# A four-layer graph network on one core: layer 1's first rows as a pipeline over four engines, and the end of layer 2 taken in steps beside layer 3

## The chip, the core and the metric

The kernel runs on one core of one Trainium2 chip. The time is the device time in microseconds of the core, median of the runs. Five engines work beside each other, each in its own program order: TensorE (PE in the profile; its weight loads are PEld), VectorE (DVE), ScalarE (ACT), GpSimd (POOL) and SyncE (SP, which issues transfers here). In the code they are `T`, `V`, `S`, `G` and `nc.sync`.

## What is computed

`x` has 4096 rows of 64, `adj` is a 4096 x 4096 matrix of zeros and ones, sparse. Four layers follow one another, each on the layer norm of `x` with its negative part cut off, and each adds its result to `x`:

```python
h = relu(layernorm(x)); x = x + layer0(h, adj)      # hyperbolic attention over the neighbours
h = relu(layernorm(x))
deg = clip(sum(adj, 1) + 1, 1)                      # layer 1
z = relu(concat([h, (adj @ h + h) / deg]) @ W1 + b1)
x = x + z / max(norm(z), 1e-12)
h = relu(layernorm(x))
for k in range(2):                                  # layer 2: two hops
    h = tanh(concat([adj @ h, h], 1) @ W2[k])
x = x + h
h = relu(layernorm(x))                              # layer 3
w = mask(adj) * 0.5 ** (how many neighbours stand to the right in the row), the last 100 of a row
x = x + w @ (h @ W3) + b3
```

The kernel multiplies by the weights first: `y = h @ W`, then `adj @ y`. Each `y` is split into three bf16 parts (value, rest, rest of the rest) that stand side by side, so a product with the 0/1 adjacency in fp8 has 3 x 64 columns and loses nearly nothing.

## The kernel before

The 4096 rows are 32 chunks of 128 rows, one chunk per partition set; eight chunks are a group, and there are four groups. `x` is 128 x 32 x 64 in SBUF. At the end of layer 0, `finish` writes the last two groups of `x`:

```python
        yield 0.35
        for g in range(g0, g1):
            rows, part = slice(g * 8, g * 8 + 8), slice((g - g0) * 8, (g - g0) * 8 + 8)
            t, s = block(f"f_t{g}"), block(f"f_s{g}")
            V.tensor_mul(t, h[:, rows, :], bc(a[:, part], D))
            V.tensor_mul(s, vs[:, rows, :D], bc(f[:, part], D))
            yield 1.4
            V.tensor_add(s, s, t)
            V.tensor_add(x[:, rows, :], x[:, rows, :], s)
            yield 1.4
```

Layer norm of a group (128 x 8 x 64, so 512 elements in each partition), used ahead of layers 1, 2 and 3, with its root:

```python
    def root(self, pool, a, n, name):
        V, S = self.nc.vector, self.nc.scalar
# [... cut: tiles s, inv, q ...]
        S.activation(s, a, AF.Sqrt)
        V.reciprocal(inv, s)
        V.tensor_mul(q, a, inv)
        V.tensor_add(q, q, s)
        V.tensor_scalar_mul(s, q, 0.5)
        V.reciprocal(inv, s)
        return s, inv
# [... cut ...]
    def ln_group(self, pool, xx, h, name, block=None):
        V, S = self.nc.vector, self.nc.scalar
        st = pool.tile([P, 8], F32, tag="ln_st", name=f"{name}_st")
# [... cut ...]
        V.tensor_reduce(st, xx, AX.X, ALU.add)
        V.tensor_scalar_mul(st, st, 1.0 / D)
        V.tensor_sub(cen, xx, st[:, :, None].to_broadcast([P, 8, D]))
        S.activation(sq, cen, AF.Square)
        var = pool.tile([P, 8], F32, tag="ln_v", name=f"{name}_v")
        V.tensor_reduce(var, sq, AX.X, ALU.add)
        V.tensor_scalar(var, var, 1.0 / D, LN_EPS, op0=ALU.mult, op1=ALU.add)
        _, inv = self.root(pool, var, 8, name)
        V.tensor_mul(cen, cen, inv[:, :, None].to_broadcast([P, 8, D]))
        V.tensor_scalar_max(h, cen, 0.0)
```

The weight product of a group, with the splitting into three parts:

```python
    def weigh(m, h, y3, w, name, bias=None):

        nw = D if w is None else w.shape[-1]
        pt = bank("t", f"{name}_t{m}").rearrange("p (k i) -> p k i", k=4)
        for k in range(4):
            T.transpose(pt[:, k, :], h[:, 2 * k : 2 * k + 2, :].rearrange("p k d -> p (k d)"), ident)
        ht = lw.tile([P, 4, P], F32, tag="ht", name=f"{name}_h{m}")
        S.copy(ht, pt)
        if nw == D:

            pu = bank("u", f"{name}_u{m}")
            for k in range(4):
                T.matmul(pu[:, k * P : (k + 1) * P], ht[:, k, :], w3_t, start=True, stop=True)
            outs = [(pu.rearrange("p (k e) -> p k e", k=GR), slice(m * GR, m * GR + GR))]
        else:
            pus = [bank("u", f"{name}_u{m}_{s}").rearrange("p (k e) -> p k e", k=4) for s in range(2)]
            for k in range(GR):
                half = slice(k % 2 * D, k % 2 * D + D)
                T.matmul(pus[k % 2][:, k // 2, :], ht[half, k // 2, :], w[half, :], start=True, stop=True)
            outs = [(pus[s], slice(m * GR + s, m * GR + GR, 2)) for s in range(2)]
        for pu, rows in outs:
            n = pu.shape[1]
            yy = pu[:, :, :D]
            S.copy(y3[:, rows, 0:D], yy)
            rest = lw.tile([P, n, D], F32, tag=f"rest{n}", bufs=8 // n, name=f"{name}_r{rows.start}")
            V.tensor_sub(rest, yy, y3[:, rows, 0:D])
            S.copy(y3[:, rows, D : 2 * D], rest)
            V.tensor_sub(y3[:, rows, 2 * D : 3 * D], rest, y3[:, rows, D : 2 * D])
            if nw > D:
                if bias is None:
                    S.copy(base[:, rows, :], pu[:, :, D:])
                else:
                    V.tensor_add(base[:, rows, :], pu[:, :, D:], along_d(bias, n))
# [... cut ...]
    def joined(acc, agg):
        V.tensor_reduce(agg, acc[:, :, : 3 * D].rearrange("p k (s d) -> p k d s", s=3), AX.X, ALU.add)

    def product(y3, cols, name, made, tail, order, done, beside, itself=False, behind={}):


        first = [c for m in made[:-1] for c in range(m * GR, m * GR + GR)]
        last = range(made[-1] * GR, made[-1] * GR + GR)
        for at, m in enumerate(order):
            agg = lw.tile([P, GR, D], F32, tag="agg", bufs=3, name=f"{name}_agg{m}")
            accs = {}

            def part(k, chunks):
# [... cut: one T.matmul(acc, adjacency of row chunk k and chunk c, y3[:, c]) for each chunk c ...]
            def end(k):
# [... cut: with `itself` the product of the identity idb with y's own chunk; then, if k is odd: ...]
                    done(m, k // 2, accs[k // 2], agg)

            if at == 0:
                for g in made[:-1]:
                    for k in range(GR):
                        part(k, range(g * GR, g * GR + GR))
                    if g in behind:
                        behind[g]()
                tail()
                for k in range(GR):
                    part(k, last)
                    end(k)
                continue
            for k in range(GR):
                part(k, first)
                part(k, last)
                end(k)
                if k == 5:
                    beside(order[at - 1])
```

`product` multiplies the adjacency with `y` for one group of output rows after another (`order`). In the first of them the chunks of `y` are taken as the groups of `y` are made: `made`, with `behind` called after a group's products, and `tail` ahead of the last group. Then the use of it. The whole block fixes the order of instructions by hand: each engine runs them in the order written.

```python
# [... cut: tri and fill of layer 3 are made here, see the diff ...]
        hs = {}
        V.memset(y3s[0][:, :, 3 * D : 3 * D + 1], 1.0)
        dgs = {}

        def first_y(m):
            weigh(m, ln_group(m, "ln1"), y3s[0], both(0), "l1", bias=b1_t)

        first_y(0)
        first_y(1)
# [... cut ...]
        product(
            y3s[0], 3 * D + 1, "l1", up, lambda: None,
            up, l1_done, lambda m: weigh(m, hs[m], y3s[1], both(1), "l2"), itself=True,
            behind={0: lambda: first_y(2), 1: lambda: first_y(3)},
        )
# [... cut ...]
        def hop(m, k2, acc, agg):
            pair = agg[:, 2 * k2 : 2 * k2 + 2, :]
            joined(acc, pair)
            V.tensor_add(pair, pair, base[:, m * GR + 2 * k2 : m * GR + 2 * k2 + 2, :])
            if k2 == GR // 2 - 1:
                S.activation(agg, agg, AF.Tanh)
                aggs[m] = agg
                return True

        def second_y(m):
            weigh(m, aggs[m], y3s[0], both(2), "l2b")

        product(
            y3s[1], 3 * D, "l2a", up, lambda: weigh(NQ - 1, hs[NQ - 1], y3s[1], both(1), "l2"), up, hop, second_y
        )

        def l2b_done(m, k2, acc, agg):
            if hop(m, k2, acc, agg):
                V.tensor_add(x[:, group(m), :], x[:, group(m), :], agg)
                hs[m] = ln_group(m, "ln3")
                V.tensor_add(x[:, group(m), :], x[:, group(m), :], along_d(b3_t, GR))

        def third_y(m):
            weigh(m, hs[m], y3s[1], None, "l3")

        product(y3s[0], 3 * D, "l2b", up, lambda: second_y(NQ - 1), down, l2b_done, third_y)
```

Layer 3 takes the rows in four quarters (`q`) of eight chunks. For every chunk `c` of columns, from the right, `cnt` counts by TensorE how many neighbours stand to the right; a weight tile (the power of two as a bit pattern) is made from each half of it, one half on VectorE and one on ScalarE; `fill` then brings the counts on for the next chunk.

```python
        def weighted(q, accs, item):
# [... cut: eight T.matmul of the weight tiles' 128-column pieces with y3[:, c] into accs ...]

        for q in range(NQ):
            accs = [bank("acc", f"l3_acc{q}_{k}", bufs=4).rearrange("p (k e) -> p k e", k=2) for k in range(4)]
            cnt = [bank("t" if b else "u", f"cnt{q}_{b}") for b in range(2)]
            pend = None
            for c in reversed(range(NCH)):
                head_, last = c == NCH - 1, c == 0
                masks = [a8[2 * q + b][:, c, :] for b in range(2)]
                for b in range(2):
                    T.matmul(cnt[b], tri, masks[b], start=head_, stop=last, skip_group_check=True)
                wts = [lw.tile([P, 512], I16, tag=f"wt{b}", bufs=3, name=f"wt{q}_{c}_{b}") for b in range(2)]
                if pend is not None:
                    weighted(q, accs, pend)
                pend = (c, wts)
                if q == 0 and c == 22:
                    third_y(0)
                V.tensor_scalar(wts[0], cnt[0], -(128.0 - MAX_NEIGH) * UNIT, 0.0, op0=ALU.add, op1=ALU.max)
                S.activation(wts[1], cnt[1], AF.Relu, bias=low_t)
                if not last:
                    for b in range(2):
                        T.matmul(cnt[b], fill, masks[b], start=False, stop=False, skip_group_check=True)
            weighted(q, accs, pend)
            rows = slice(q * GR, (q + 1) * GR)
            agg = lw.tile([P, GR, D], F32, tag="agg", bufs=3, name=f"l3_agg{q}")
            for k2 in range(4):
                joined(accs[k2], agg[:, 2 * k2 : 2 * k2 + 2, :])
            z = lw.tile([P, GR, D], F32, tag="sq", name=f"z3_{q}")
            V.scalar_tensor_tensor(z, agg, 2.0**27, x[:, rows, :], op0=ALU.mult, op1=ALU.add)
            nc.sync.dma_start(out[:, rows, :], z)
```

## Time and profile before

| what | value |
|---|---|
| time, median of 3 runs | 947.08 us (944.4 to 957.32) |
| span of the profiled execution | 943.8 us |
| layer 0 ends, layer 1 begins | 360 us |
| layer 1's first row block ends | 422 us |
| layer 2 begins, second hop, layer 3 | 497, 598, 698 us |

The profile page has shares of busy time for each engine, the span in 40 slices, groups of instructions, and the chain of work that ended last. Beside it the trace can be asked for stretches (busy time of each engine between two times, with the clock granted to TensorE as a share of its full speed, the share of time in which the transfer engines were busy, and GB/s) and for the timeline. A line of the timeline is: start in us, length in us, engine, line of the kernel before, operation, out<-in by the names of the tiles, shapes, count, and in brackets the idle time of the engine before it and what ended it. Lines L1743 to L1752 are the layer norm, L1725 to L1732 its root, L1467 to L1494 `weigh`, L1501 `joined`, L1520 and L1529 `product`, L1649 to L1680 layer 3.

### The profile page before, as it was taken

The numbers are of one execution on the slowest core, as the hardware profiler recorded it, in microseconds if no ns is written. First come the engines' busy times: TensorE is split into PE (matmuls) and PEld (weight loads), VectorE is DVE, ScalarE is ACT, GpSimd is POOL, SyncE is SP. The second block draws the span as 40 slices with busy tenths as digits, with TensorE's granted clock in tenths as the row PEclk, the third lists the DMA queues.
The fourth block names the chain that finished last, engine by engine and source line by source line (L and its number), as shares of the span: only waits on it lengthen the run. The fifth ranks groups of instructions, "written<-read, shape, count | busy, mean of one in ns | idle before, by whom it ended". The sixth has DMA issues, their size and how long they took to land.

```text
span 943.8 us, 15045 instructions
## 1 busy us (share of the span) xinstructions
PE 770.2 (82%) x6076; PEld 576.1 (61%) x6096; DVE 518.1 (55%) x1496; ACT 343.3 (36%) x471; POOL 167.6 (18%) x178
## 2 busy tenths in 40 slices
PE   4767765986898751789998999989958989989896
PEld 1323333733637331679998999989955656656564
DVE  4668777776889976445555222144443344444443
ACT  4766566574631332211112011122223334434342
POOL 0337766176277100000000000000000000000000
PEclk9879897798998985799999899999988899999999
DMA  8889999899711006300000000000000000000000
GB/s 285 309 309 324 377 354 350 293 364 340 267 38 28 8 1 288 158 1 1 1 2 1 1 1 1 2 1 2 1 1 1 1 12 1 2 12 1 12 2 15
DMA packets 48225, 98.39 MB, mean 104 GB/s; under 512 B 6290, under 2 KB 6290, under 8 KB 47250
## 3 DMA queue, kind: packets, MB, share of 16 engines
q1 hardware_dynamic: 35232, 79.70, 23.5%
q10 hardware_dynamic: 7794, 11.98, 3.4%
q0 software_dynamic: 5120, 5.66, 2.8%
q8 instruction: 49, 0.80, 0.3%
q14 instruction: 30, 0.25, 0.1%
HBM read 84.66 MB, written 12.67 MB: 103 GB/s over the span
## 4 chain that ended last, share of the span: by engine, by line
PE 66%; DMA 12%; DVE 10%; ACT 9%; issue 2%; ACTq 0%; SPq 0%
PE l2a_acc L1520 9%; PE l2b_acc L1520 9%; PE l_acc L1649 9%; PE l_acc L1520 8%; PE cnt L1673 7%; DMA adj<-f 7%; PE cnt L1662 6%; PE fill_t L1117 4%; ACT f L796 3%; PE v L1131 3%; PE pk L801 2%; DMA a<-in_adj_t 2%; PE v L1124 2%; ACT a L793 1%; PE l_u L1480 1%
## 5 line engine op out<-in xcount | busy, mean ns | idle before, releaser
L1520 PEld LDWEIGHTS <-a 128*128 128x128 fp8e4 x3072 | 264.8, 99 | 9.2 <-issue 6.9
L1669 DVE TENSOR_SCALAR wt<-cnt 128x512 int16<-128x512 f32 x128 | 88.5, 691 | 123.4 <-PE cnt L1662 123.4
L997 POOL DMA_INDIRECT es<-rows_d,idx x128 | 126.7, 989 | 98.7 <-issue 36.3
L1670 ACT ACTIVATE wt<-cnt,low_t 128x512 int16<-128x512 f32 x128 | 88.0, 687 | 137.2 <-PE cnt L1662 137.2
L1649 PEld LDWEIGHTS <-wt 128*128 128x128 bf16 x1024 | 90.1, 99 | 31.7 <-issue 2.5
L1649 PE MATMUL l_acc<-y_b,wt 128*128 128x192 bf16 x1024 | 107.8, 249 | 0.0
L1117 PE MATMUL fill_t<-io,wpack 128*128 128x512 bf16 x298 | 93.8, 406 | 13.5 <-DVE hw L971 7.3
L1673 PE MATMUL cnt<-a,fill 128*128 128x512 fp8e4 x248 | 82.2, 387 | 20.3 <-DVE wt L1669 20.0
L1520 PE MATMUL l_acc<-y_a,a 128*128 128x193 bf16 x1024 | 93.9, 252 | 0.0
L796 ACT CAST f<-a 128x2048 fp8e4<-128x2048 f32 x40 | 75.8, 1896 | 47.5 <-DMA adj<-f 45.9
L1520 PE MATMUL l2a_acc<-y_b,a 128*128 128x192 bf16 x1024 | 89.4, 250 | 3.0 <-DVE y_b L1489 3.0
L1520 PE MATMUL l2b_acc<-y_a,a 128*128 128x192 bf16 x1024 | 88.2, 248 | 3.0 <-DVE y_a L1489 3.0
L801 PE MATMUL pk<-a,wpack 128*128 128x512 bf16 x248 | 74.1, 420 | 16.6 <-DMA a<-in_adj_t 16.1
L1662 PE MATMUL cnt<-a,tri 128*128 128x512 fp8e4 x256 | 78.0, 387 | 0.0
L1117 PEld LDWEIGHTS <-wpack 128*128 128x128 bf16 x310 | 31.3, 104 | 65.0 <-issue 36.1
L801 PEld LDWEIGHTS <-wpack 128*128 128x128 bf16 x256 | 26.9, 108 | 50.0 <-issue 17.4
L811 PE MATMUL keys<-ident,kt 128*128 128x128 f32 x64 | 14.7, 371 | 49.3 <-ACT kt L807 49.3
L793 ACT CAST a<-a 128x2048 fp8e4<-128x2048 f32 x24 | 45.0, 1898 | 12.0 <-DMA a<-in_adj_t 7.7
L1662 PEld LDWEIGHTS <-tri 128*128 128x128 bf16 x256 | 25.0, 98 | 38.2 <-issue 23.2
L811 PEld LDWEIGHTS keys<-ident,kt 128*128 128x128 f32 x64 | 9.4, 184 | 57.5 <-ACT kt L807 57.5
L1673 PEld LDWEIGHTS <-fill 128*128 128x128 bf16 x248 | 24.2, 98 | 28.0 <-issue 21.3
L1467 PE MATMUL l_t<-ident,ln_h 128*128 128x128 f32 x48 | 8.3, 301 | 38.0 <-DMA a<-adj 23.2
(376 smaller groups left out, 890.9 us busy)
## 6 DMA issues: line engine op xcount, KB each, us to landing
a<-in_adj_t SPq DMA_DIRECT2D x64, 1024.0 KB, 7.6
adj<-f ACTq DMA_DIRECT2D x40, 256.0 KB, 5.9
a<-adj SPq DMA_DIRECT2D x5, 2048.0 KB, 16.5
es<-rows_d,idx POOLq DMA_INDIRECT x128, 5.3
rows_d<-tab ACTq DMA_DIRECT2D x1, 1104.0 KB
x<-in_x SPq DMA_DIRECT2D x1, 1024.0 KB
out<-z SPq DMA_DIRECT2D x4, 256.0 KB, 2.0
es<-rows_d,ovx POOLq DMA_INDIRECT x32, 5.5
```

The source lines that it names most:

```text
L793: S.copy(a8[b][:, 4 * at : 4 * at + 4, :], a, saturate=False)
L796: S.copy(f8, a, saturate=False)
L801: T.matmul(pk, wflat[:, w * P : (w + 1) * P], bits[:, j, :, 1], start=(w == 0), stop=(w == 15),)
L997: G.indirect_dma_start(out=dst, out_offset=None, in_=rows_d, in_offset=bass.IndirectOffsetOnAxis(ap=at, axis=0))
L1117: T.matmul(fill_t, wflat[:, :P], fill_in, start=True, stop=True, skip_group_check=True)
L1131: T.matmul(pv[:, k * DQ : (k + 1) * DQ], spot[nb][:, c, k * P : (k + 1) * P], es[g][:, q, LB * NS + c, :DQ], start=False, stop=(c == NO - ...
L1520: T.matmul(acc, a8[n // 4][:, c, n % 4 * P : (n % 4 + 1) * P], y3[:, c, :cols], start=(c == first[0] and k % 2 == 0), stop=(c == last[-1] ...
L1649: T.matmul(accs[k // 2][:, k % 2, : 3 * D], wts[k // 4][:, (k % 4) * P : (k % 4 + 1) * P].bitcast(BF16), y3[:, c, : 3 * D], start=(c == NC ...
L1662: T.matmul(cnt[b], tri, masks[b], start=head_, stop=last, skip_group_check=True)
L1669: V.tensor_scalar(wts[0], cnt[0], -(128.0 - MAX_NEIGH) * UNIT, 0.0, op0=ALU.add, op1=ALU.max)
L1670: S.activation(wts[1], cnt[1], AF.Relu, bias=low_t)
L1673: T.matmul(cnt[b], fill, masks[b], start=False, stop=False, skip_group_check=True)
```

## The change

It does four things. In layer 1 the layer norms of the four groups are laid out as a pipeline: VectorE makes the sums, GpSimd centres and scales groups 1 to 3, ScalarE squares and cuts the negative part, and the weight products of groups 1 to 3 are taken in steps amid the first products with the adjacency, so that TensorE need not wait for a whole group's norm. `weigh` becomes a generator of such steps (`weighing`) and splits both halves of a group beside each other. The last group of layer 2 is closed in steps beside the first chunks of layer 3; while they run, ScalarE makes both weight tiles, and also in the first two chunks of the later quarters. At the end of layer 0 two of the last products go to GpSimd, and the set-up of layer 3's tiles moves behind layer 1. In the diff only changed lines are shown; `...` stands for unchanged ones.

```diff
--- before.py
+++ after.py
@@ -1260,7 +1260,7 @@
-            V.tensor_mul(t, h[:, rows, :], bc(a[:, part], D))
+            (G if g1 == NQ else V).tensor_mul(t, h[:, rows, :], bc(a[:, part], D))
@@ -1444,7 +1444,6 @@
-    V.tensor_copy(idb, ident)
@@ -1459,6 +1458,11 @@
+        for _ in weighing(m, h, y3, w, name, bias):
+            pass
+    def weighing(m, h, y3, w, name, bias=None):
@@ -1467,6 +1471,7 @@
+        yield
@@ -1479,19 +1484,25 @@
+        yield
+        rests = []
...
-            yy = pu[:, :, :D]
-            S.copy(y3[:, rows, 0:D], yy)
+            S.copy(y3[:, rows, 0:D], pu[:, :, :D])
...
-            V.tensor_sub(rest, yy, y3[:, rows, 0:D])
+            V.tensor_sub(rest, pu[:, :, :D], y3[:, rows, 0:D])
+            rests.append(rest)
+            if nw == D:
+                yield
+        for rest, (pu, rows) in zip(rests, outs):
...
-            if nw > D:
-                if bias is None:
-                    S.copy(base[:, rows, :], pu[:, :, D:])
-                else:
-                    V.tensor_add(base[:, rows, :], pu[:, :, D:], along_d(bias, n))
+        if nw > D:
+            for pu, rows in outs:
+                S.copy(base[:, rows, :], pu[:, :, D:])
+            if bias is not None:
+                G.tensor_add(base[:, group(m), :], base[:, group(m), :], along_d(bias, GR))
+        yield
@@ -1500,7 +1511,7 @@
-    def product(y3, cols, name, made, tail, order, done, beside, itself=False, behind={}):
+    def product(y3, cols, name, made, tail, order, done, beside, itself=False, amid={}):
@@ -1535,10 +1546,11 @@
+                    steps = amid.get(g)
...
-                    if g in behind:
-                        behind[g]()
+                        if steps is not None and k > 0:
+                            next(steps, None)
@@ -1555,27 +1567,64 @@
-        tri_f = res.tile([P, P], F32, name="tri_f")
-        tri = res.tile([P, P], BF16, name="tri")
-        fill_f = res.tile([P, P], F32, name="fill_f")
-        fill = res.tile([P, P], BF16, name="fill")
-        low_t = res.tile([P, 1], F32, name="low_t")
-        V.memset(low_t, -(128.0 - MAX_NEIGH) * UNIT)
-        V.tensor_scalar(tri_f, diff, 0.0, -UNIT, op0=ALU.is_lt, op1=ALU.mult)
-        V.scalar_tensor_tensor(tri, ident, 128.0 * UNIT, tri_f, op0=ALU.mult, op1=ALU.add)
-        V.tensor_scalar(fill_f, diff, 0.0, -UNIT, op0=ALU.is_gt, op1=ALU.mult)
-        V.scalar_tensor_tensor(fill, ident, -129.0 * UNIT, fill_f, op0=ALU.mult, op1=ALU.add)
...
-        def first_y(m):
-            weigh(m, ln_group(m, "ln1"), y3s[0], both(0), "l1", bias=b1_t)
-        first_y(0)
-        first_y(1)
+        cens = [lw.tile([P, GR, D], F32, tag="ln_h", name=f"ln1_c{m}") for m in range(2)]
+        cens += [lw.tile([P, GR, D], F32, tag="agg", bufs=3, name=f"ln1_c{m}") for m in range(2, NQ)]
+        sqs = [lw.tile([P, GR, D], F32, tag=tag, name=f"ln1_s{m}") for m, tag in enumerate(["ln_b", "ln_b", "sq", "sq"])]
+        def means(m0, m1, eng):
+            n = (m1 - m0) * GR
+            st = lw.tile([P, n], F32, tag=f"st{n}", name=f"ln1_st{m0}")
+            sum_d(st, x[:, m0 * GR : m1 * GR, :])
+            V.tensor_scalar_mul(st, st, 1.0 / D)
+            for m in range(m0, m1):
+                at = slice((m - m0) * GR, (m - m0) * GR + GR)
+                eng.tensor_sub(cens[m], x[:, group(m), :], over_d(st[:, at], GR))
+        def squares(m0, m1):
+            for m in range(m0, m1):
+                S.activation(sqs[m], cens[m], AF.Square)
+        def scales(m0, m1, eng):
+            n = (m1 - m0) * GR
+            var = lw.tile([P, n], F32, tag=f"var{n}", name=f"ln1_v{m0}")
+            for m in range(m0, m1):
+                sum_d(var[:, (m - m0) * GR : (m - m0) * GR + GR], sqs[m])
+            V.tensor_scalar(var, var, 1.0 / D, LN_EPS, op0=ALU.mult, op1=ALU.add)
+            _, inv = root(lw, var, n, f"ln1_{m0}")
+            for m in range(m0, m1):
+                at = slice((m - m0) * GR, (m - m0) * GR + GR)
+                eng.tensor_mul(cens[m], cens[m], over_d(inv[:, at], GR))
+        def relus(m0, m1):
+            for m in range(m0, m1):
+                S.activation(cens[m], cens[m], AF.Relu)
+        ys = [weighing(m, cens[m], y3s[0], both(0), "l1", bias=b1_t) for m in range(NQ)]
+        means(0, 1, V)
+        squares(0, 1)
+        means(1, 2, G)
+        scales(0, 1, V)
+        squares(1, 2)
+        relus(0, 1)
+        next(ys[0])
+        means(2, NQ, G)
+        next(ys[0])
+        scales(1, 2, G)
+        squares(2, NQ)
+        relus(1, 2)
+        for _ in ys[0]:
+            pass
+        V.tensor_copy(idb, ident)
+        scales(2, NQ, G)
+        def second_weights():
+            yield from ys[1]
+            relus(2, NQ)
@@ -1605,8 +1654,20 @@
-            behind={0: lambda: first_y(2), 1: lambda: first_y(3)},
+            amid={0: second_weights(), 1: ys[2], 2: ys[3]},
...
[... cut: the set-up of tri and fill removed above, unchanged ...]
@@ -1627,14 +1688,45 @@
+        closing = []
...
-            if hop(m, k2, acc, agg):
+            if m == 0 and k2 == GR // 2 - 1:
+                closing.append(closing_steps(m, k2, acc, agg))
+            elif hop(m, k2, acc, agg):
...
+        def closing_steps(m, k2, acc, agg):
+            rows = group(m)
+            hop(m, k2, acc, agg)
+            yield True
+            V.tensor_add(x[:, rows, :], x[:, rows, :], agg)
+            st, var = (lw.tile([P, GR], F32, tag=f"{t}{GR}", name=f"ln3_{t}") for t in ("st", "var"))
+            sum_d(st, x[:, rows, :])
+            V.tensor_scalar_mul(st, st, 1.0 / D)
+            yield True
+            cen = lw.tile([P, GR, D], F32, tag="ln_h", name="ln3_c")
+            sq = lw.tile([P, GR, D], F32, tag="ln_b", name="ln3_s")
+            V.tensor_sub(cen, x[:, rows, :], over_d(st, GR))
+            S.activation(sq, cen, AF.Square)
+            yield True
+            sum_d(var, sq)
+            V.tensor_scalar(var, var, 1.0 / D, LN_EPS, op0=ALU.mult, op1=ALU.add)
+            yield True
+            _, inv = root(lw, var, GR, "ln3")
+            V.tensor_mul(cen, cen, over_d(inv, GR))
+            yield True
+            V.tensor_scalar_max(cen, cen, 0.0)
+            V.tensor_add(x[:, rows, :], x[:, rows, :], along_d(b3_t, GR))
+            yield True
+            for _ in weighing(m, cen, y3s[1], None, "l3"):
+                yield False
@@ -1664,9 +1756,12 @@
-                if q == 0 and c == 22:
-                    third_y(0)
-                V.tensor_scalar(wts[0], cnt[0], -(128.0 - MAX_NEIGH) * UNIT, 0.0, op0=ALU.add, op1=ALU.max)
+                busy = next(closing[0], False) if q == 0 else c > NCH - 3
+                if busy:
+                    S.activation(wts[0], cnt[0], AF.Relu, bias=low_t)
+                else:
+                    V.tensor_scalar(wts[0], cnt[0], -(128.0 - MAX_NEIGH) * UNIT, 0.0, op0=ALU.add, op1=ALU.max)
```

## The prediction

> **What bounds the kernel now.** I read the page first, for the shares of the engines:
>
> ```profile
> PE 770.2 (82%) x6076; PEld 576.1 (61%) x6096; DVE 518.1 (55%) x1496; ACT 343.3 (36%) x471; POOL 167.6 (18%) x178
> ```
>
> TensorE (PE) is busiest, but 82% is a mean over stages, so I asked next for the busy time in stretches that follow the code (columns: stretch, its length, busy us of each engine, then the clock granted to TensorE).
>
> ```profile
> 374.00:382.00 8.00, 1.11 (x4) 0.71 (x4) 5.10 (x14) 1.22 (x3) 0.00 (x0) 0.50 1.03 439
> 382.00:395.00 13.00, 10.06 (x84) 9.10 (x84) 6.62 (x18) 3.01 (x8) 0.00 (x0) 0.76 0.31 132
> 395.00:409.00 14.00, 9.82 (x98) 9.04 (x100) 6.61 (x18) 2.95 (x8) 0.00 (x0) 0.87 0.00 1
> 420.00:497.00 77.00, 74.81 (x882) 73.73 (x881) 41.48 (x113) 12.79 (x33) 0.00 (x0) 1.00 0.01 2
> 694.00:716.00 22.00, 12.70 (x98) 9.07 (x96) 10.54 (x23) 7.30 (x11) 0.00 (x0) 0.77 0.00 1
> ```
>
> The reader is to see that layer 1 from 420 us on is bound by TensorE (74.81 of 77 us, clock 1.00), and that its start and the seam between layers 2 and 3 are not: there TensorE waits and then runs at half clock. So a saved wait there moves everything behind it. The timeline gives the waits:
>
> ```profile
> 380.47 1.11 PE L1467 MATMUL l_t<-ident,ln_h 128*128 128x128 f32 x4 [9.46 <-DVE ln_h L1752]
> 384.27 7.38 PE L1520 MATMUL l_acc<-y_a,a 128*128 128x193 bf16 x64
> 393.73 0.66 PE L1467 MATMUL l_t<-ident,ln_h 128*128 128x128 f32 x4 [2.08 <-DVE ln_h L1752]
> 406.59 0.66 PE L1467 MATMUL l_t<-ident,ln_h 128*128 128x128 f32 x4 [3.32 <-DVE ln_h L1752]
> ...
> 708.03 1.01 PE L1673 MATMUL cnt<-a,fill 128*128 128x512 fp8e4 x2 [9.30 <-DVE wt L1669]
> 730.43 1.01 PE L1673 MATMUL cnt<-a,fill 128*128 128x512 fp8e4 x2 [3.38 <-DVE wt L1669]
> 772.86 0.59 PE L1673 MATMUL cnt<-a,fill 128*128 128x512 fp8e4 x2 [2.44 <-DVE wt L1669]
> ```
>
> L1520 is a product with the adjacency, L1467 the transposes ahead of the weight products, L1673 the `fill` product of layer 3. Products of the first row block begin only at 384.27, although y of group 0 was ready at 374.46: by program order TensorE stands behind group 1's transposes, which wait 9.46 us for group 1's layer norm, nearly all of it on VectorE. The block ends at 422.1. At 708.03 and 730.43 `fill` waits for a weight tile that VectorE makes only after the layer norm, or the last y conversion.
>
> [...] granted 0.50 from 365 to 388 us, 0.99 in 388 to 390, that is 4 us after the products began; after the 9.3 us wait it was 0.50 until about 712. So each removed wait also removes a cold stretch.
>
> [...]
>
> ```profile
> 28.01 0.69 DVE L732 TENSOR_TENSOR cens<-cens,ln_i 128x512 f32<-128x512 f32 x1
> 30.60 1.19 POOL L738 TENSOR_TENSOR cens<-tab,wl_t 128x512 f32<-128x512 f32 x1
> 31.28 1.05 DVE L732 TENSOR_TENSOR cens<-cens,ln_i 128x512 f32<-128x512 f32 x1
> ```
>
> The VectorE product takes 0.69 us alone and 1.05 us when it meets the GpSimd one: it ends 0.54 us after GpSimd's end at 31.79. GpSimd needs 1.19 us for what VectorE does in 0.69.
>
> [...] Relu at 704.42 follows a Sqrt with no table load. So the Relus moved to ScalarE bring no loads of 1.28 us (the trace's duration).
>
> **Part 1, layer 1's start.** Walk through the new order with the trace's durations (128x512: VectorE product 0.69, reduction 0.69, GpSimd 1.19, ScalarE 0.63; about 0.05 us from engine to engine).
>
> End of layer 0: two of eight products go to GpSimd. [...] 354.5 + 6 x 0.6 (VectorE's pitch) + 2 x 1.19 = 360.5, against 359.9. I book a loss of 0.6, not a gain.
>
> Group 0: the six small instructions for `tri`, `fill` and `idb` (359.92 to 361.04) are moved away, saving 1.1. Memset, sum, scale, centring end at 362.2; square 362.85; the table load for Sqrt to 364.15; the variance's last step may be held by GpSimd's centring of group 1 to 364.4; root 365.75; scaling 366.5; Relu on ScalarE 367.15 (0.63 for VectorE's 0.43). Transposes at 367.2, as before (367.17); weight products end at 371.1 at half clock (1.1 + 0.6 + 2.1).
>
> The splitting of y0 then stands on ScalarE behind Relu of group 1. That chain: sums of groups 2 and 3 on VectorE to 367.95, variance of group 1 with GpSimd centring beside it to 369.4, [...] scaling on GpSimd 372.6, Relu 373.3. Splitting in the new order (two casts, two differences, two casts, two differences, from the trace 0.37, 0.42, 0.41, 0.43 and pitches of 0.31 to 0.35) takes 2.15: y0 is ready at 375.5. Products begin there, 8.8 us before 384.27.
>
> From there nothing should wait: each group gives eight packets of eight products, and the next group's transposes, weight products and splitting hang between the packets. y1 is ready about 9 us after the start (two packets 2.7 at half clock, transposes 1.1, packet 1.2, weight products 1.8, splitting 2.3), and group 0's packets last 10.5. TensorE's own work: 8 x 2.805 us (the pitch of 32 products plus the identity one, from 422 us on) = 22.4; three times transposes and weight products 3 x 1.76 = 5.3; half clock for about 4.5 us costs 2.3. Sum 30.0, end at 405.5, against 422.1: gain 16.6. For small unseen waits I take 16.
>
> **Part 2, the tails of layers 2a and 2b.** The new splitting order also serves the last group, on which TensorE waits alone: after the weight products end at 515.41 it does one product at 517.23 and goes on at 518.67. In the new order all is split 2.15 us after the end: 517.55. Gain 1.1, twice 2.2. If the shorter gap keeps the clock (0.50 from 518 to 524 now), there is up to 2 more; I book 0.3. Sum 2.5.
>
> **Part 3, the seam to layer 3.** Now the first Tri product is at 698.06 and that of chunk 18, where the rhythm of 1.64 us is back, at 738.36: 40.3 us for 13 chunks, whose rhythm would be 21.3. In the new order ScalarE makes both weight tiles in six chunks. First chunk: reduction, sum and Tanh end at 699.89 as now, then two Relus of 0.69: `fill` ends at 701.47, so 3.4 us. A busy chunk then runs: Tri product, 0.42 to the first Relu, two Relus to 1.75, second `fill` to 2.0. Five of them 10.0, and one holds the table load and Sqrt, of which 0.65 fits in ScalarE's gap: 0.8 more. VectorE's norm runs ahead beside this. Then the steps of the weight product: transposes with the copy ahead of the Relu on ScalarE 3.45; weight products 2.85; two splitting steps 2.1 and 1.7. Chunks 21 to 19 run at the rhythm, 4.9. Sum 3.4 + 10.0 + 0.8 + 10.1 + 4.9 = 29.2[...]. Gain 40.3 - 29.2 = 11.1; I take 10 for a clock that may dip.
>
> **Part 4, between the row quarters of layer 3.** Three times `fill` waits 2.44 us for VectorE, which sums the finished quarter first (four reductions 1.95, the addition 0.69). Now Tri to Tri is 3.46; with both tiles on ScalarE 2.05, and the next chunk 0.4 above its rhythm: gain 1.0 each, 3.0. One gap of the three now goes cold and loses about 1.4; I book 0.5. Sum 3.5.
>
> Sum: 16 + 2.5 + 10 + 3.5 = 32. From 947.1 this gives 915.
>
> **Rivals.** [...] GpSimd holds VectorE back more than I booked. Against it: only six GpSimd instructions of 1.19 us lie before the first product (two in layer 0's end, four in layer 1), and a VectorE reduction was not slowed beside one (0.69 at 30.68). If each cost its whole length once more, y0 would be 7 us later: 922. Second, ScalarE becomes the bound: its Relu of groups 1 to 3 ahead of y's casts, or both weight tiles plus the closing work in a chunk. The window 716 to 770 has it 20.94 of 54 us busy, so there is room, but order matters and not the sum. If every seam chunk took 3 us instead of 2, six us are lost: 921. Third, the adjacency's second part, in flight from 360 to 387 us, becomes the wait once products start earlier. Against: the first row block reads the resident part, and row block 1 would begin at 405, 18 us after the last byte; nothing lost. Fourth, the clock: intermittent work at the seam keeps TensorE at half speed, half of part 3 and 2 us of part 1 gone: 922. All at once would be near 935.
>
> **Range and chances.** The parts are counted from durations, so the uncertainty is in waits: I put 12 to 18 for part 1, 6 to 12 for part 3, 3 to 8 for the rest. The three runs before spread from 944.4 to 957.3, which adds some us. I expect 915 us, 905 to 926 in 8 of 10. Two per cent is 928; it takes two rivals together to miss it: 0.88 faster, 0.09 within, 0.03 slower.
>
> **What would show it.** Products of layer 1 begin 8 to 9 us earlier (about 375), their first row block ends near 405 without a wait over 1 us; VectorE instructions of 0.69 us stretch to over 1 us beside GpSimd; layer 0's end is no earlier; no `fill` wait of 9 us remains, but some ten of 0.4; quarter gaps shrink to about 1 us. I'm wrong if the row block waits for y1 or y2, if a table load stands at each seam chunk, or if the clock is 0.50 through the seam.

## The result, and the profile after

| | before | after |
|---|---|---|
| time, median of 4 runs | 945.74 us (942.31 to 957.32) | 909.66 us (905.76 to 911.43) |
| span of the profiled execution | 943.8 us | 904.0 us |

The ratio is 0.9624, 95% interval 0.9575 to 0.9674: the changed kernel is 3.8% faster. By the medians the gain is 36.1 us, by the two profiled executions 39.8; the profiled execution of after is the fastest of its four.

The page of the kernel after, shares of the engines:

```profile
PE 759.9 (84%) x6076; PEld 567.6 (63%) x6096; DVE 498.9 (55%) x1456; ACT 353.0 (39%) x494; POOL 181.5 (20%) x190
```

TensorE has the same 6076 instructions and is busy 10.3 us less: half-clock time has gone (it is busy at half clock for 98.6 us before and for 74.4 after, by the clock records of the two traces). ScalarE and GpSimd are busy 9.7 and 13.9 us longer. Where the 40 us come from is read from milestones of the two traces. All times below are counted **from the end of layer 0** (its last addition ends at 359.89 us before and 361.02 after), since layer 0's length varies by some us from run to run. A tail is the place in each hop of layer 2 where TensorE waits for the last group's `y`; the seam is the passage from layer 2 to layer 3; Tri is the product with `tri` that opens each chunk of layer 3.

| stretch | before | after | gain | booked |
|---|---|---|---|---|
| layer 0's last eight blocks of 128x512 | 5.40 | 6.01 | -0.6 | -0.6 |
| end of layer 0 to the first product of layer 1 | 24.38 | 13.35 | 11.0 | } 16.6 |
| first product to the end of the first row block | 37.86 | 29.40 | 8.5 | |
| rest of layer 1 | 74.74 | 74.74 | 0.0 | 0 |
| layer 2, first hop and second hop | 201.27 | 196.22 | 5.0 | 2.5 |
| seam: first Tri product of layer 3 to that of chunk 18 | 40.22 | 28.91 | 11.3 | 10 |
| rest of layer 3 | 205.40 | 200.32 | 5.1 | 3.5 |

The rows below the first sum to 40.9 us. The end of layer 0 lies 1.1 us later (the 0.6, and 0.5 in where those blocks begin), so the span falls by 39.8.

The kernel after in stretches (stretch, length, busy us of PE, PEld, DVE, ACT and POOL with counts, granted clock, share of transfers, GB/s):

```profile
361.00:374.00 13.00, 3.20 (x20) 2.50 (x20) 9.58 (x27) 6.93 (x14) 4.12 (x4) 0.50 0.93 376
374.00:404.00 30.00, 29.53 (x326) 28.09 (x327) 9.61 (x29) 9.53 (x27) 7.10 (x6) 0.93 0.45 189
404.00:478.00 74.00, 71.81 (x848) 70.74 (x845) 40.29 (x111) 12.57 (x33) 0.00 (x0) 1.00 0.01 2
674.00:704.00 30.00, 25.27 (x173) 16.28 (x171) 12.67 (x25) 16.39 (x26) 0.00 (x0) 0.94 0.00 1
```

From the first product to the end of the row block TensorE is now busy 29.53 of 30 us; before, its stretches there were busy 10.06 of 13 and 9.82 of 14. The stretch of layer 1 that was already bound by TensorE is unchanged. The seam is the only stretch of these where TensorE still waits after it has begun.

The timeline of the kernel after, from layer 0's end into layer 1:

```profile
355.01 0.69 DVE L1264 TENSOR_TENSOR f_s<-vs,f_f 128x512 f32<-128x512 f32 x1
355.04 2.58 POOL L1263 TENSOR_TENSOR f_t<-tab,f_a 128x512 f32<-128x512 f32 x2 [42.80 <-DVE f_f L1258]
356.65 1.52 DVE L1266 TENSOR_TENSOR f_s<-f_s,f_t 128x512 f32<-128x512 f32 x1 [0.94 <-POOL f_t L1263]
...
363.61 1.04 POOL L1586 TENSOR_TENSOR ln_c<-x,ln_st 128x512 f32<-128x512 f32 x1 [5.99 <-issue]
364.10 0.58 DVE L1597 TENSOR_SCALAR ln_v<-ln_v 128x8 f32<-128x8 f32 x1
...
369.23 2.08 PE L1485 MATMUL l_u<-wab,l_h 64*128 64x128 f32 x16 [0.67 <-ACT l_h L1473]
...
372.07 0.63 ACT L1605 ACTIVATE ln_c<-ln_c 128x512 f32<-128x512 f32 x1 [1.22 <-POOL ln_c L1601]
372.60 0.63 ACT L1491 CAST y_a<-l_u 128x256 bf16<-128x256 f32 x2
...
374.37 2.91 PE L1531 MATMUL l_acc<-y_a,a 128*128 128x193 bf16 x16 [3.06 <-DVE y_a L1499]
...
377.08 1.06 PE L1471 MATMUL l_t<-ident,ln_c 128*128 128x128 f32 x4
...
384.71 0.60 PE L1471 MATMUL l_t<-ident,ln_c 128*128 128x128 f32 x4
...
391.91 0.60 PE L1471 MATMUL l_t<-ident,ln_c 128*128 128x128 f32 x4
```

Three things are to be seen. At 356.65 VectorE's addition takes 1.52 us where the next one (359.60) takes 0.69: it runs beside the second of GpSimd's two products, which ends at 357.62, and ends 0.55 us after it. (The first took 1.57 us, beside VectorE's own product of 355.01, and the second 1.04.) At 364.10 a VectorE step on 128 x 8 values, 0.17 us at 363.31, takes 0.58 and ends 0.03 us after GpSimd's centring, which ends at 364.65. And y0 is split at 372.60 only when ScalarE has made the Relu of group 1; the first product follows at 374.37. The transposes of groups 1 to 3 (L1471 at 377.08, 384.71 and 391.91) carry no bracket: TensorE has not been idle ahead of any of them.

The timeline of the kernel after, TensorE at the seam and at the first turn between quarters:

```profile
677.11 0.38 PE L1768 MATMUL cnt<-a,fill 128*128 128x512 fp8e4 x1 [1.78 <-ACT wt L1762]
...
686.50 0.38 PE L1768 MATMUL cnt<-a,fill 128*128 128x512 fp8e4 x1 [0.63 <-ACT wt L1762]
...
692.25 0.38 PE L1768 MATMUL cnt<-a,fill 128*128 128x512 fp8e4 x1 [1.05 <-ACT wt L1765]
...
736.21 0.38 PE L1768 MATMUL cnt<-a,fill 128*128 128x512 fp8e4 x1 [0.56 <-ACT wt L1762]
736.78 0.38 PE L1768 MATMUL cnt<-a,fill 128*128 128x512 fp8e4 x1 [0.20 <-ACT wt L1765]
```

The wait of 9.30 us for VectorE's tile has become one of 1.78 in the first chunk and then several of 0.2 to 1.05, and the releaser is now ScalarE's Relu (L1762, L1765). At the turn of a quarter 2.44 us have become 0.56 and 0.20.

And the seam, cut where its clock changes, kernel after (the number ahead of the last two is the clock):

```profile
675.17:678.58 3.41, 1.43 (x9) 0.63 (x7) 2.58 (x6) 2.05 (x4) 0.00 (x0) 1.00 0.00 0
678.58:681.99 3.41, 3.41 (x17) 2.23 (x16) 1.13 (x3) 2.62 (x5) 0.00 (x0) 0.50 0.00 0
681.99:685.40 3.41, 3.21 (x25) 1.99 (x24) 0.00 (x0) 2.46 (x4) 0.00 (x0) 1.00 0.00 0
```

Here the clock falls to 0.50, and TensorE's longest gap ahead of that was 1.78 us. This comes back below.

### The profile page after: what moved, and what is told of

Same layout as the page of the kernel before. It is cut to its first block, busy times and chain, and to the rows that moved or that the text cites. A ratio compares the mean times of both kernels' runs of the same rounds, so it can differ in the third digit from the quotient of the medians.

```text
span 904.0 us, 15063 instructions
## 1 busy us (share of the span) xinstructions
PE 759.9 (84%) x6076; PEld 567.6 (63%) x6096; DVE 498.9 (55%) x1456; ACT 353.0 (39%) x494; POOL 181.5 (20%) x190
## 4 chain that ended last, share of the span: by engine, by line
PE 62%; DMA 15%; ACT 11%; DVE 8%; issue 2%; ACTq 1%; POOL 0%; DVEq 0%; POOLq 0%
DMA adj<-f 11%; PE l_acc L1531 10%; PE l2b_acc L1531 10%; PE l2a_acc L1531 10%; PE l_acc L1741 9%; PE cnt L1768 7%; PE cnt L1754 6%; ACT f L796 5%; PE fill_t L1117 3%; DMA a<-in_adj_t 2%; PE v L1131 2%; ACT a L793 1%; PE v L1124 1%; ACT wt L1765 1%; PE l_u L1485 1%
## 5 line engine op out<-in xcount | busy, mean ns | idle before, releaser
L1531 PEld LDWEIGHTS <-a 128*128 128x128 fp8e4 x3072 | 260.8, 98 | 9.4 <-issue 4.3
L1764 DVE TENSOR_SCALAR wt<-cnt 128x512 int16<-128x512 f32 x116 | 80.2, 692 | 113.7 <-PE cnt L1754 113.7
L1765 ACT ACTIVATE wt<-cnt,low_t 128x512 int16<-128x512 f32 x128 | 87.8, 686 | 110.0 <-PE cnt L1754 110.0
L1531 PE MATMUL l2a_acc<-y_b,a 128*128 128x192 bf16 x1024 | 86.6, 246 | 1.9 <-DVE y_b L1499 1.8
L1754 PEld LDWEIGHTS <-tri 128*128 128x128 bf16 x256 | 24.6, 96 | 40.8 <-issue 25.1
L1512 DVE TENSOR_REDUCE l2a_agg<-l2a_acc 128x128 f32<-128x384 f32 x16 | 8.9, 558 | 53.3 <-PE l2a_acc L1531 53.3
L997 POOL DMA_INDIRECT es<-rows_d,ovx x32 | 30.2, 945 | 15.8 <-issue 7.3
```

The lines of the kernel that those rows point to most:

```text
L997: G.indirect_dma_start(out=dst, out_offset=None, in_=rows_d, in_offset=bass.IndirectOffsetOnAxis(ap=at, axis=0))
L1531: T.matmul(acc, a8[n // 4][:, c, n % 4 * P : (n % 4 + 1) * P], y3[:, c, :cols], start=(c == first[0] and k % 2 == 0), stop=(c == last[-1] ...
```

## The experiments

The theory: the gain is the sum of independent waits of TensorE removed (the pipeline at layer 1, the steps at the seam, the order of splitting, the quarter turns), each behind which everything moves up. The rivals: that one part carries nearly all, that the sharing with GpSimd is what helps (or what holds back), that the clock and not the waits makes the difference, that the transfer in flight slows layer 1's start. e1, e2, e3 and e5 undo one part each; e4 and e6 put one part's work back on VectorE; e7, e8 and e10 to e12 add to the change, and e9 repeats it. They ran on several chips; on two of them layer 0 ends 45 to 60 us later (before takes 1000.04 and 1002.45 us there), so stages are compared from the end of layer 0 and whole times only as ratios to the kernel before on the same chip.

### e1: without the pipeline

The changed kernel, but layer 1's first rows as before: one group's whole norm and weight product after another, and groups 2 and 3 behind the products of groups 0 and 1. The set-up of layer 3's tiles stays moved and the splitting order stays new.

```diff
-        ys = [weighing(m, cens[m], y3s[0], both(0), "l1", bias=b1_t) for m in range(NQ)]
-        means(0, 1, V)
# ... the whole laid-out order of norms
+        def first_y(m):
+            weigh(m, ln_group(m, "ln1"), y3s[0], both(0), "l1", bias=b1_t)
+        first_y(0)
+        V.tensor_copy(idb, ident)
+        first_y(1)
-            amid={0: second_weights(), 1: ys[2], 2: ys[3]},
+            behind={0: lambda: first_y(2), 1: lambda: first_y(3)},
```

> The changed kernel with layer 1's start as before (norm of a whole group on VectorE, then its weights, groups 0 and 1 ahead of the first products, 2 and 3 behind them). Theory (each wait removed at layer 1's start moves everything behind it): the first row block ends about 18 us later against the start of layer 1 than in the changed kernel, nothing of it is given back, so about 928 us against 909.7, ratio to the kernel before about 0.981. Rival (the later stages' gains come from the earlier start, for instance the clock kept through the tail): more than 18 us are lost, or the tail of layer 2a goes cold again and costs 2.8 us more. Second rival (the pipeline's gain is partly hidden by what follows): fewer than 14 us are lost.

Measured: 924.61 us (922.69 to 928.81), ratio to before 0.9759 (0.9686 to 0.9832). The first product comes 22.45 us after layer 0's end (after: 13.35), the row block ends at 57.57 (42.75). The timeline of this kernel:

```profile
381.60 1.12 PE L1471 MATMUL l_t<-ident,ln_h 128*128 128x128 f32 x4 [8.60 <-DVE ln_h L1799]
...
385.40 6.20 PE L1531 MATMUL l_acc<-y_a,a 128*128 128x193 bf16 x64
```

The wait of group 1's transposes is back, 8.60 us, and with it the start of the products behind them. The pipeline is worth 57.57 - 42.75 = 14.8 us at the end of the row block and 15.0 at the end of the kernel. (In between two differences of the clock nearly cancel: e1 loses it in the first hop, 99.09 us against 97.46, and keeps it at the seam, 28.09 against 28.91.) That is between what the theory and the rival expected: of the 62.24 - 42.75 = 19.5 us gained at layer 1's start, 4.7 are there without the pipeline. The set-up moved away (1.1 us) and the shorter splitting are two sources of it; the 64 products here also take 6.20 us against 7.38 before, since the clock rises 1.3 us after their start (at 386.66) and not 3.8 (before, at 388.03).

### e2: without the steps at the seam

```diff
-            if m == 0 and k2 == GR // 2 - 1:
-                closing.append(closing_steps(m, k2, acc, agg))
-            elif hop(m, k2, acc, agg):
+            if hop(m, k2, acc, agg):
-                busy = next(closing[0], False) if q == 0 else c > NCH - 3
+                busy = q > 0 and c > NCH - 3
+                if q == 0 and c == 22:
+                    third_y(0)
```

> The changed kernel with the last group of layer 2 closed at once and its weights at chunk 22, as before; the rest as changed. Theory: the stretch from the first Tri product of layer 3 to chunk 18 is 40 us again instead of 28.9, so about 921 us, ratio to before about 0.974; waits of 9.3 and 3.4 us are back and with them two cold stretches. Rival (layer 3's first chunks are bound by something else, say ScalarE with both tiles, and part of the gain was luck with the clock): the stretch is 35 us or less.

Measured: 915.92 us (915.15 to 924.18), ratio 0.9681 (0.9601 to 0.9761). In the trace the seam is 40.17 us long, as before (40.22), and layer 3 240.52 against 229.23. Its timeline:

```profile
684.14 1.01 PE L1768 MATMUL cnt<-a,fill 128*128 128x512 fp8e4 x2 [9.30 <-DVE wt L1764]
...
706.50 1.01 PE L1768 MATMUL cnt<-a,fill 128*128 128x512 fp8e4 x2 [3.38 <-DVE wt L1764]
```

Both waits return to the hundredth (9.30 and 3.38). The steps are worth 11.3 us. The medians differ by 6.3 only, but on ranges of 9 and 6 us; the profiled spans differ by 10.8 (914.8 and 904.0). From the end of layer 0 everything up to layer 3 is equal to 0.04 us, so the parts don't interact.

### e3: the splitting in its old order

```diff
+        if nw > D:
+            for pu, rows in outs:
+                S.copy(y3[:, rows, 0:D], pu[:, :, :D])
+                V.tensor_sub(rest, pu[:, :, :D], y3[:, rows, 0:D])
+                S.copy(y3[:, rows, D : 2 * D], rest)
+                V.tensor_sub(y3[:, rows, 2 * D : 3 * D], rest, y3[:, rows, D : 2 * D])
+                S.copy(base[:, rows, :], pu[:, :, D:])
```

> The changed kernel with the old order of splitting (one half of a group wholly before the other, the copies to base between). Theory: in the tails of layers 2a and 2b the products go on 4.4 us after the weight products begin instead of 3.3, so 1.1 us later each; layer 1's first products begin about 1 us later. [...] Rival (the order of splitting decides over the clock): both tails go cold, as it was cold after both in the kernel before, and each costs over 2.5 us.

Measured: 914.18 us (one run). The timeline of this kernel, where layer 2's first hop waits for its last group:

```profile
500.01 1.16 PE L1485 MATMUL l_u<-wab,l_h 64*128 64x128 f32 x16 [0.73 <-ACT l_h L1473]
502.98 0.32 PE L1544 MATMUL l2a_acc<-y_b,a 128*128 128x192 bf16 x1 [1.81 <-DVE y_b L1495]
504.43 5.81 PE L1544 MATMUL l2a_acc<-y_b,a 128*128 128x192 bf16 x39 [1.12 <-DVE y_b L1495]
```

The same place in the timeline of the kernel after:

```profile
495.89 1.16 PE L1485 MATMUL l_u<-wab,l_h 64*128 64x128 f32 x16 [0.73 <-ACT l_h L1473]
498.86 4.34 PE L1531 MATMUL l2a_acc<-y_b,a 128*128 128x192 bf16 x47 [1.81 <-DVE y_b L1499]
```

In the old order one product fits in and the second wait of 1.12 us follows; in the new one the products run on (both lines are cut off where the window ends). From the weight products to the run of products it is 4.42 us against 3.30 (495.89 to 498.86, and one product on), twice in layer 2. The rest is clock: after the old tail it is 0.50 from 502.6 to 509.5 us, and 39 products take 5.81 us where 47 take 4.34. The first hop lasts 100.95 us against 97.46, the second 99.71 against 98.76, and the row block of layer 1 ends 1.8 us later. Its first product was expected 1 us later too and is not (13.34 us after layer 0's end against 13.35): it needs the first half of `y` alone, which both orders make first; the next product then waits 1.09 us in e3. The order is worth 1.1 per tail for certain; whether the clock survives the tail is looked at under e11 and at the end.

### e4: layer 0's last blocks on VectorE

```diff
-            (G if g1 == NQ else V).tensor_mul(t, h[:, rows, :], bc(a[:, part], D))
+            V.tensor_mul(t, h[:, rows, :], bc(a[:, part], D))
```

> The changed kernel with the two products at the end of layer 0 on VectorE again. Theory [...]: the time from the last small instruction of layer 0 to the end of its last addition is 5.4 us instead of 6.0, so about 0.6 to 0.7 us faster. Rival (GpSimd takes work off VectorE): 0.7 us or more slower, 6.7 us or more from one to the other.

Measured: 904.91 us (one run). The eight blocks last from 352.60 to 357.99 = 5.39 us, against 6.01 with two of them on GpSimd: the 0.6 us are there, to the digit. This part of the change costs time. The whole time can't show it: the end of layer 0 moves more than that between runs.

### e5: the quarter turns as before

```diff
-                busy = next(closing[0], False) if q == 0 else c > NCH - 3
+                busy = next(closing[0], False) if q == 0 else False
```

> The changed kernel with the first two weight tiles of quarters 1 to 3 of layer 3 on VectorE again (the steps at the seam stay). Theory: Tri to Tri at each of the three turns is 3.46 us instead of 1.95 and the next chunk 1.64 instead of 1.95, so 1.2 us more for each turn, 3.6 in all, and up to 2 us more where the gap of 2.4 us goes cold. Rival (ScalarE's two tiles cost as much as VectorE's wait saves): under 2 us in all.

Measured: 965.2 us where before takes 1000.04 (one run). Layer 3 lasts 232.71 us against 229.23. The timeline of this kernel at the first turn:

```profile
790.88 0.59 PE L1754 MATMUL cnt<-a,tri 128*128 128x512 fp8e4 x2
...
793.92 0.59 PE L1768 MATMUL cnt<-a,fill 128*128 128x512 fp8e4 x2 [2.44 <-DVE wt L1764]
```

The 2.44 us are back and Tri to Tri is 3.47 us (790.88 to 794.35). Three turns give 3.5 us in all, where 1.2 each was expected.

### e6: layer 1's norms on VectorE, in the same order

```diff
-        means(1, 2, G)
+        means(1, 2, V)
-        means(2, NQ, G)
+        means(2, NQ, V)
-        scales(1, 2, G)
+        scales(1, 2, V)
-        scales(2, NQ, G)
+        scales(2, NQ, V)
```

> The changed kernel with GpSimd's centring and scaling of groups 1 to 3 on VectorE (0.69 us each instead of 1.04). Theory ([...] the pipeline's gain is in the order and not in the fourth engine): the first products of layer 1 begin at most 0.6 us later against the end of layer 0, and the first row block ends at most 1 us later. Rival (GpSimd takes four times 0.69 us off the path ahead of the first product): first products about 2.8 us later, and the row block waits for y2 or y3.

Measured: 961.06 us where before takes 1000.04 (one run). The first product comes 13.88 us after layer 0's end against 13.35, the row block ends at 44.28 against 42.75. The timeline of this kernel:

```profile
427.26 2.91 PE L1531 MATMUL l_acc<-y_a,a 128*128 128x193 bf16 x16 [3.27 <-DVE y_a L1499]
```

The wait ahead of the first products is 3.27 us where it is 3.06 after. So GpSimd's share of the pipeline is worth 0.5 us at the first product, and the other 1.0 of the 1.5 at the end of the row block, where at most 1 was expected, lies behind it, in products at half clock (eight take 1.50 us; the clock comes up 19.9 us after layer 0's end, and 17.2 in the kernel after). So at least 13.3 of the 14.8 us of e1 are there without the fourth engine: they come from the order of the instructions. The small VectorE steps that take 0.48 to 0.58 us beside GpSimd in the kernel after (0.17 each here), and GpSimd's longer durations (1.04 us a block against 0.69), nearly eat up what GpSimd takes over.

### e7: products that keep the array busy

The changed kernel with seven products of the identity with data that is there anyway, f32, 128 x 512, whose result nobody reads: five ahead of the first transposes, two after the weight products of group 0.

```diff
+        warm = bank("acc", "warm", bufs=4)
+        for _ in range(5):
+            T.matmul(warm, ident, x[:, group(2), :].rearrange("p k d -> p (k d)"), start=True, stop=True)
+        for _ in range(2):     # after next(ys[0]) has made the weight products
+            T.matmul(warm, ident, sqs[1].rearrange("p k d -> p (k d)"), start=True, stop=True)
```

> The changed kernel with seven products added whose result nobody reads: five of the identity with a group of x ahead of the first transposes of layer 1, two between the first weight products and the first products with the adjacency. Theory (the first 4 us of layer 1 are slow for the cold clock only): transposes 0.6 instead of 1.1 us, weight products 1.2 instead of 2.1, the first 16 products 1.4 instead of 2.9; the row block, 29.4 us from first product to end now, takes 27.1. Rival (they are slow because of the transfer of the adjacency in flight until 387 us): the first 16 products still take 2.5 us or more though the clock reads 1.00.

Measured: 950.48 us where before takes 1000.04 (one run); row block 42.48 us after layer 0's end against 42.75. The timeline of this kernel:

```profile
412.61 0.65 PE L1471 MATMUL l_t<-ident,ln_c 128*128 128x128 f32 x4 [1.48 <-ACT ln_c L1605]
413.94 1.16 PE L1485 MATMUL l_u<-wab,l_h 64*128 64x128 f32 x16 [0.68 <-ACT l_h L1473]
415.03 1.98 PE L1612 MATMUL warm<-ln_s,ident 128*128 128x512 f32 x4
419.54 2.92 PE L1531 MATMUL l_acc<-y_a,a 128*128 128x193 bf16 x16 [2.53 <-DVE y_a L1499]
```

And its stretches:

```profile
414.00:416.00 2.00, 2.00 (x19) 1.40 (x20) 1.59 (x6) 1.34 (x3) 1.36 (x2) 1.00 1.01 434
418.00:420.00 2.00, 0.46 (x3) 0.24 (x4) 1.70 (x6) 1.69 (x6) 0.02 (x1) 0.82 0.98 418
420.00:422.00 2.00, 2.00 (x14) 1.87 (x13) 1.65 (x5) 0.22 (x1) 1.25 (x1) 0.50 0.95 410
```

It worked in half. The transposes take 0.65 us instead of 1.12 and the weight products 1.16 instead of 2.08, with the transfer engines fully busy beside them (1.01): so it was the clock, not the transfer, that made them slow. But the fillers end at 417.0, y0 is ready only at 419.5, and the clock falls just before (419.28), in a gap of 2.5 us: the first 16 products take 2.92 us as they did without any filler. The time ahead of y0 is set by VectorE, GpSimd and ScalarE, so the faster weight products bring nothing there. What was expected of the row block wasn't reached.

### e8: smaller steps at the seam

The closing work is cut in smaller pieces (the root's parts, the sums and each splitting step apart), each placed after both weight tiles of a chunk and not ahead of them; VectorE makes its tile again.

```diff
+            S.activation(s, var, AF.Sqrt)
             yield
-            _, inv = root(lw, var, GR, "ln3")
+            V.reciprocal(inv, s)
# ... the root's other steps, then a yield; likewise the other closing steps
-                busy = next(closing[0], False) if q == 0 else c > NCH - 3
+                busy = q > 0 and c > NCH - 3
# ... both weight tiles of the chunk ...
+                if q == 0 and c < NCH - 1:
+                    next(closing[0], None)
```

> The changed kernel with the closing of layer 2 in smaller steps placed behind each chunk's two weight tiles, one tile on VectorE and one on ScalarE throughout. Theory (in the changed kernel the seam's chunks take 2.0 us and more because ScalarE makes both tiles one after the other, with the steps in front of them): each chunk is back at 1.64 us but for the first (about 2.6), the one with the table load (about 0.5 more) and the weight products (1.8), so 24.6 us from the first Tri product to chunk 18 instead of 28.9. Rival (VectorE has no room for tile and step within a chunk, which was why ScalarE took both): 28 us or more.

Measured: 955.04 us where before takes 1000.04 (one run). The seam lasts 24.15 us (729.10 to 753.25) against 28.91, close to the 24.6 of the theory, and layer 3 is 5.3 us shorter. The timeline of this kernel:

```profile
733.28 0.59 PE L1762 MATMUL cnt<-a,tri 128*128 128x512 fp8e4 x2
...
734.87 0.59 PE L1762 MATMUL cnt<-a,tri 128*128 128x512 fp8e4 x2
...
736.51 0.59 PE L1762 MATMUL cnt<-a,tri 128*128 128x512 fp8e4 x2
```

After the first chunk (2.59 us) five follow at 1.59 to 1.64 us, the rhythm, where those of the changed kernel take 2.0 to 3.2; of the seven later ones four, with the root and the weight product among their steps, take 1.96 to 2.44. The clock is 1.00 from 729 to 753. So the two Relus in a row on ScalarE were not needed: the closing work fits between the tiles if each piece is short.

### e9 and e10: the changed kernel again, and all of it together

e9 is the changed kernel without an edit, beside the kernel before on one chip. e10 puts layer 0's end back on VectorE, has the seam of e8, ends the busy turn of a quarter one chunk earlier, splits y0 ahead of the Relu of group 1 and the squares, and has fillers as in e7 and two more in the tail of layer 2.

```diff
-        squares(2, NQ)
-        relus(1, 2)
         for _ in ys[0]:
             pass
+        relus(1, 2)
+        squares(2, NQ)
# in weighing, for the last group:
+        if m == NQ - 1 and name != "l1":
+            warm = bank("t", f"{name}_warm")
+            for n in (512, 256):
+                T.matmul(warm[:, :n], ident, ht.rearrange("p k d -> p (k d)")[:, :n], start=True, stop=True)
```

> The changed kernel once more, unaltered, as the yardstick for the run beside it. Every theory: the ratio to the kernel before is again 0.962, give or take half a per cent; from the end of layer 0 the first products begin after 13.35 us, the first row block ends after 42.7, layer 3 begins after 313 to 317 (by the clock in the tails) and ends after 543 to 546.

> The changed kernel with what the runs so far point to: the two products at the end of layer 0 on VectorE; the splitting of y0 on ScalarE ahead of group 1's Relu and of the squares of groups 2 and 3; products without a reader that keep the array busy ahead of layer 1's first transposes, ahead of its first products and in the tails of layers 2a and 2b; the smaller steps at the seam, one weight tile on each engine; at the quarters only the first chunk's two tiles on ScalarE. Theory (what is left at these places is order on ScalarE and cold clock): end of layer 0 0.6 us earlier, first products 11.2 us after it instead of 13.35, the row block 27.1 us long instead of 29.4, layers 2a and 2b 97.4 us each with the clock at 1.00 through both tails, the seam to chunk 18 24.2 instead of 28.9, quarters 0.3 us shorter each: 11 to 13 us in all, ratio to before about 0.949 to 0.951 where the changed kernel has 0.962. Rival ([...] filling the waits does not hold it): the row block and the tails stay as they are, and 7 us are gained, ratio 0.955.

Measured: e9 966.16 us (965.24 to 967.59), ratio to before 0.9634 (0.9596 to 0.9672); e10 953.69 us (948.08 to 957.09), ratio 0.9489 (0.9449 to 0.9529). The result repeats, and the version with all steps is faster than the changed kernel. But its fillers misfired at layer 1's start. The timeline of e10:

```profile
417.88 5.93 PE L1616 MATMUL warm<-x,ident 128*128 128x512 f32 x10 [13.36 <-DVE x L1267]
426.90 0.66 PE L1471 MATMUL l_t<-ident,ln_c 128*128 128x128 f32 x4 [3.09 <-ACT ln_c L1609]
428.23 2.08 PE L1485 MATMUL l_u<-wab,l_h 64*128 64x128 f32 x16 [0.68 <-ACT l_h L1473]
430.24 3.78 PE L1616 MATMUL warm<-ln_s,ident 128*128 128x512 f32 x4
```

The five fillers (the trace has two records for each of these f32 products, x10 in all) end at 423.8, 3.1 us before the transposes. The clock falls behind that gap, at 427.53, when the transposes have just ended at full clock (0.66); the weight products take 2.08 us again, and the two later fillers take 3.78 us instead of 1.98 and end when y0 has long been ready. So the first product is no earlier (13.43 us after layer 0's end) than in e9 (13.35).

### e11 and e12: fillers without a gap, and none

e11 is e10 with four fillers at first and three more, which take the squares of group 0 as their data and so start later. e12 is e10 without any filler.

```diff
-        warming(x[:, group(2), :], 5)
+        warming(x[:, group(2), :], 4)
# ... means and scales of group 0 ...
+        warming(sqs[0], 3)
```

> The run with all steps, but its products without a reader spread differently ahead of layer 1: four on a group of x and three on the squares of group 0, so that no wait of 3 us stays ahead of the first transposes. Theory ([...] in the run before a wait of 3.1 us turned it cold, and the fillers themselves then took 3.8 instead of 2.0 us and held up the first products): with the clock at 1.00 through, the first products begin 11.4 us after the end of layer 0 instead of 13.4 and the row block ends after 38.6 instead of 41.3. Rival (the fillers stand in the way whatever the clock): first products at 13 us or later.

> The run with all steps, without any product that has no reader. Theory (order on ScalarE alone lets y0 follow its weight products at once, and the cold clock costs the rest): first products 12.7 us after the end of layer 0 (transposes at 6.5, 1.1 + 0.7 + 2.1 at half clock, 2.3 for the splitting), row block ends after 42, l2a 97.5 to 100 and l2b 98.6 us. Rival (y0 waits for GpSimd or VectorE whatever ScalarE's order is): first products at 13.3 us as in the changed kernel.

Measured on one chip, where before takes 947.95 us: e11 901.45 us (891.25 to 905.7), ratio 0.9441 (0.9376 to 0.9505); e12 901.45 us (899.44 to 903.09), ratio 0.9488 (0.944 to 0.9535). From the end of layer 0, in us:

| | first product | row block | end of layer 1 | end of first hop | end |
|---|---|---|---|---|---|
| after (e9) | 13.35 | 42.52 | 117.26 | 214.72 | 542.53 |
| e10 | 13.43 | 41.26 | 116.00 | 213.46 | 534.77 |
| e11 | 11.45 | 40.06 | 114.80 | 212.26 | 533.63 |
| e12 | 12.24 | 42.51 | 117.25 | 216.10 | 537.60 |

The timeline of e11:

```profile
374.67 1.16 PE L1485 MATMUL l_u<-wab,l_h 64*128 64x128 f32 x16 [0.67 <-ACT l_h L1473]
375.76 1.98 PE L1616 MATMUL warm<-ln_s,ident 128*128 128x512 f32 x4
378.27 1.77 PE L1535 MATMUL l_acc<-y_a,a 128*128 128x193 bf16 x16 [0.53 <-DVE y_a L1503]
```

And of e12:

```profile
373.20 2.91 PE L1531 MATMUL l_acc<-y_a,a 128*128 128x193 bf16 x16 [1.86 <-DVE y_a L1499]
```

With no gap over 0.7 us the clock stays at 1.00 from 370 us on in e11, and the first 16 products take 1.77 us instead of 2.91. The first product comes when it was expected; the row block ends 1.5 us later than the 38.6 expected, with one wait of 0.80 us in it ahead of group 1's weight products. By the traces the fillers are worth 2.5 us at the end of the row block and 4.0 at the end. By the whole times they are not to be told from nothing: the medians are equal and the intervals overlap, since layer 0 ended at 366.82 us in e11's profiled execution and at 360.96 in e12's. Of e12's gain over the changed kernel the seam is shown by itself (24.15 us). Splitting y0 ahead of Relu and squares brings the first product 1.1 us earlier (13.35 to 12.24), but the row block ends no earlier (42.51 against 42.52): the clock comes up 18.0 us after layer 0's end and not 16.6 as in e9.

The tails of layer 2. In the old splitting order the first hop's clock was lost in both traces that have it (before 101.38 us, e3 100.95). In the new order without fillers it was kept in six of ten traces (97.46 or 97.47: after, e2, e5, e7, e8, e9) and not in four (98.85 to 100.14: e1, e4, e6, e12), though the instructions are the same (the wait is 1.81 us in the kernel after); the last section sets one of each side by side. With the fillers of e10 and e11 it was kept in both (97.46, 97.47). In the second hop the clock was lost in every trace without fillers. With them it reads 98.44 us and not 97.46, at a clock of 1.00, because the filler also stands in one weight product of layer 3 that lies in this hop, an oversight that costs about 1 us.

## Why the prediction was right, step by step

The time, 909.66 us, lies in the range and 5 us under the middle; the order of the parts is as predicted, and no rival came to more than a us or two. Undone one at a time, the pipeline (14.8 us), the seam's steps (11.3), the turns (3.5) and the splitting order in two tails (2.2) make up 31.8 of the 40.9 us gained behind layer 0. The rest is 4.7 us of layer 1's start that are there without the pipeline, and clock. By the terms of the sum:

- **End of layer 0, booked as a loss of 0.6:** 6.01 against 5.40 us, and e4 takes it back (5.39). The sum was right to a tenth, its items less so: GpSimd's products took 1.57 and 1.04 us where 1.19 each was booked, and VectorE's addition waited 0.94 us for the first and then took 1.52 us beside the second (0.69 for the next one).
- **Part 1, booked 16:** 19.5 from the end of layer 0 to the end of the row block, less the 0.6. The first product came 13.35 us after layer 0's end, not 15.0. Group 1's Relu was done after 11.7 us and not 12.8, the difference being spread over several steps (among them GpSimd's blocks with the mean or the root as an operand, 1.04 us and not the 1.19 assumed from another line), and the product starts when the first half of y0 is split, not both. The 30.0 us for the row block were 29.4 (3.8 us at half clock, 4.5 booked). That nothing would wait from there on was right, no wait over 1 us. What the working credited to the pipeline as a whole is 14.8 by e1; the rest is there without it. And e6 shows that GpSimd's share of the pipeline is 0.5 us of that at the first product.
- **Part 2, booked 2.5:** measured 5.0. The term of 1.1 per tail was exact (4.42 to 3.30). The 0.3 for the clock was mis-sized: 2.8 in the first hop of the profiled execution. That is luck: the same tail keeps the clock in six of ten traces, and where it does not the hop is 1.4 to 2.7 us longer.
- **Part 3, booked 10 of 11.1:** 28.91 us against the 29.2 worked out. Its terms have no half clock in them, and that did not hold: the clock was 0.50 from 678.58 to 681.99, with no gap over 1.78. It cost 0.8 us, for e1 and e4 have the same seam with the clock at 1.00 and take 28.09. So the working was 1.1 us too long where the clock held (the first chunk took 3.17 us, not 3.4, and a busy one 1.95, not 2.0), and the two errors nearly cancelled. "Some ten waits of 0.4" was nearly so. What the working did not see is that the change's own design was not the best one: two Relus make a chunk some 0.3 us longer (1.95 us against 1.64 at a turn), and e8 does without them at the seam. (The first Tri product of before starts at 698.14; 698.06 is its weight load.)
- **Part 4, booked 3.5:** 5.1. A turn is 1.95 us Tri to Tri (2.05 predicted), e5 puts 3.5 us on the three turns, and the rest is the cold stretch of one turn that no longer comes (1.4, booked at 0.5).
- **Rivals:** VectorE did take longer beside GpSimd, by 0.3 to 0.4 us on each of three small steps (0.48 to 0.58 against 0.17) and by 0.83 on one addition, against 7 us in that rival. ScalarE did become what TensorE waits for at the seam (L1762, L1765), at 0.2 to 1.05 us a chunk, not a us more than booked in every chunk. The adjacency's transfer held nothing up: in e7 the weight products take 1.16 us, at a clock of 1.00, with the transfers at 1.01. The clock took its toll at the seam, 0.8 us of the 7 of that rival.

The booked sum was 32 and the traces give 39.8: the margins I took off for unseen waits (0.6 and 1.1 us) and for the clock (part 2, part 4) were not used. Some of that is luck with the clock, as said under part 2.
